# Adding a kernel's residual input by an accumulating DMA, and starting the B and C products one slot earlier

## The chip, the cores and the metric

The kernel runs on one core of a Trainium2 chip. The metric is the device time of one execution in microseconds (us). A core has five engines that run their own queues in order: TensorE (PE in the profile, with PEld for its weight loads), VectorE (DVE), ScalarE (ACT), GpSimd (POOL) and SyncE (SP), which here only issues transfers. They meet at semaphores.

## The reference

The input `x` has the shape (4, 512, 64, 64) in float32: 4 batches, 512 channels, 4096 positions. Two layers follow each other, each of the form `x = x + layer(group_norm(x))`:

```python
# layer 0: mamba
xn = layer_norm(gn(x))                      # tokens of 512 channels, as 4 chunks of 128
xi, z = split(in_proj(chunk))               # 256 inner channels
xc = silu(causal_conv4(xi) + conv_b)
dt, B, C = x_proj(xc);  dt = softplus(dt_proj(dt) + dt_b)
h[t] = exp(dt[t] * A) * h[t-1] + dt[t] * xc[t] * B[t]      # 256 channels x 16 states
y = ((h * C).sum(states) + xc * D) * silu(z)
x = x + proj(layer_norm(out_proj(y) + skip * chunk)) + proj_b
# layer 1: linear attention, 8 heads
q, k, v = qkv(gn(x));  q, k = relu(q), relu(k)
kq = k.T @ q;  x = x + out_proj(v @ kq / kq.sum())
```

The addition that the change is about is the first `x +` (line "x = x + proj(...)"): the input of layer 0 is added to the projection's output. The group norm of layer 1 needs mean and variance of each channel of the sum over all positions, so statistics of the sum are collected as it is made.

## The kernel before

**Tiling.** The positions of a batch are cut into 8 tiles of 512 (index t), the channels into 4 chunks of 128 (index c). One *step* is a batch, tile and chunk: 128 steps. A step has 16 *slots* (index s), 2048 in all. In each slot `slot` (L578 on) writes out: on GpSimd the product `bx` for the slot after next (`drive`, L584), on VectorE two scans along the 512 positions (L602), each on 128 rows that hold 32 channels by 4 states, on ScalarE two exponentials `dA` for the scans to come (`decay`, L576), and on VectorE the product of the states with C for the first 384 positions (`product`, L625). Every second slot GpSimd copies the states on (L612) and multiplies the last 128 positions (L613), and TensorE makes the next `c_all` (the C values spread over the rows, `c_row`, a matmul into the only bank of its pool) and sums the states into `y` (`fold_states`).

**Pieces.** Everything else is cut into generators, and `after()`, at the end of each slot, lets some of them go on by a piece. The order is written by this loop when the program is built, not found at run time. `later(n, what)` issues `what` n slots later; `pause(n)` and `until(...)` yield until then. The queues `ahead` (layer norm of the next tile), `late` (the projection of the tile before) and `rest` (attention of the batch before) advance as long as a credit of TensorE work allows: 3.5 units a slot, a unit being a matmul of 512 columns in float32; `mm` counts them, bfloat16 as a quarter, and four small ones side by side as one.

**Banks.** The pool `ps_w` has 4 PSUM banks, used in rotation by all these pieces (`work_bank`). A matmul into a bank waits until the last reader of the tile before in that bank is done.

**Projection.** `projected` (L413 on), one call per tile, runs mostly in the slots of the steps with c = 2 and 3. After the layer norm it takes a tile buffer, one of three, and loads the 1 MiB of `x` into it from DRAM over SyncE (`load_x`, L130, tile name `xr`). For each of the 4 output chunks o it issues 4 matmuls with `w_pr` into a bank `pp` and then the *fold*: four 32x32 matmuls with an identity (`fold`) side by side, which add `xr` into the same bank. Two slots later ScalarE copies the bank plus bias over `xr` (L421), and a slot after that VectorE takes `bn_stats` of it (L423). Then the tile is stored to a DRAM tile `x1` (L442).

**Mixers.** `mixers` makes a step's B, C and time values from the SiLU output: one bank `pd` with two matmuls, the copy `dtr` and the bfloat16 `parts` (L518, L526), then twice a small correction matmul on the same bank and a copy (L531). These are six pieces; the last one reads `pd` for the last time. In before they run in slots 12 to 15 of one step and slots 0 and 1 of the next. In slot 1 `time_banks` issues the two matmuls `pt`, which need two banks, and in slot 2 ScalarE does the softplus. In slot 10 ScalarE does the SiLU of the step after next, with a table load on either side.

Of the kernel before, what the change touches and what calls it, by code (L numbers as in the profile page):

```python
# [8 lines left out]
F32 = mybir.dt.float32  # L9
BF16 = mybir.dt.bfloat16  # L10
AF = mybir.ActivationFunctionType
ALU = mybir.AluOpType
AX = mybir.AxisListType

P = 128
T = 512
# [8 lines left out]
def kernel(  # L25
# [24 lines left out]
    nc = tc.nc  # L50
    B, C, L = x.shape
    NC = C // P
# [6 lines left out]
    BLK = 32  # L59
# [6 lines left out]
    wk = ctx.enter_context(tc.tile_pool(name="wk", bufs=2))  # L66
# [19 lines left out]
    def later(n, what):  # L86

        done = []

        def both():  # L90
            what()
            done.append(True)

        if now[0] is None:
            both()
        else:
            due.append((now[0] + n, both))
        return done

    def until(*done):  # L100
        while not all(done):
            yield "wait"

    def pause(n):
        return until(later(n, lambda: None))
# [8 lines left out]
    def cols(v, b):  # L114
        return v[b].rearrange("(c p) l -> p c l", p=P)

    def mm(out_, lhsT, rhs, abreast=1, **how):

        work["mm"] += (0.25 if rhs.dtype == BF16 else 1.0) * rhs.shape[-1] / T / abreast
        nc.tensor.matmul(out_, lhsT, rhs, **how)  # L120
# [3 lines left out]
    def no_tile(spare=0):  # L124
        return now[0] is not None and held_x[0] + spare >= TILES

    def load_now(src, name):
        held_x[0] += 1
        xt = wk.tile([P, NC, T], F32, tag="x", name=name, bufs=TILES)
        nc.sync.dma_start(xt, src)  # L130
        return xt

    def load(src, name):

        while no_tile():
            yield "wait"
        return load_now(src, name)

    TILES = 3
    held_x = [0]  # L140
# [4 lines left out]
    def load_x(b, t, why):  # L145
        return load(cols(x, b)[:, :, t * T : (t + 1) * T], f"x{why}_{b}_{t}")
# [26 lines left out]
    for i in range(1, 4):  # L173
        r = slice(i * LANE, (i + 1) * LANE)
# [10 lines left out]
    fold = const.tile([P, BLK], F32, tag="fold", name="fold")  # L185
    for k in range(KS):
        r = slice(k * BLK, (k + 1) * BLK)
# [47 lines left out]
    for e in range(NH):  # L235
        r = e * (LANE + NST)
# [25 lines left out]
    for i in (2, 3):  # L262
        r = slice(i * LANE, P)
# [16 lines left out]
    for o in range(NC):  # L280
        pw = work_bank(f"pw_{o}")
        for c in range(NC):
            mm(
                pw[:, 0:1], w_pr[:, c, o * P : (o + 1) * P], b_sb[:, c : c + 1],
                start=(c == 0), stop=(c == NC - 1),
# [127 lines left out]
    def projected(ym, stats, x1, b, t):  # L413

        nm = f"{b}_{t}"
        yield from layer_norm(ym, f"b_{nm}", False)
        xt = yield from load_x(b, t, "r")
        taken = []

        def take(o, pp):  # L420
            nc.scalar.activation(xt[:, o, :], pp, AF.Identity, bias=pb[:, o : o + 1])  # L421
            free()
            later(1, lambda: nc.vector.bn_stats(stats[:, o, t, :], xt[:, o, :]))  # L423

        for o in range(NC):
            yield from room()
            pp = work_bank(f"pp_{nm}_{o}")
            for c in range(NC):
                mm(
                    pp, w_pr[:, c, o * P : (o + 1) * P], ym[:, c, :],  # L430
                    start=(c == 0), stop=False,
                )
                if c == 1:
                    yield "more"
            for k in range(P // BLK):
                r = slice(k * BLK, (k + 1) * BLK)
                mm(pp[r, :], fold[r, :], xt[r, o, :], abreast=P // BLK, start=False, stop=True)
            taken.append(later(2, lambda o=o, pp=pp: take(o, pp)))
            yield
        yield from until(*taken)  # L440
        yield from pause(1)
        nc.sync.dma_start(x1, xt)  # L442
        later(2, free_x)

# [520 lines left out]
    with tc.manual_schedule():  # L965
        credit, seen, mix, held[0], held_x[0] = 0.0, work["mm"], iter(()), 0, 0
        for n, (b, t, c) in enumerate(steps):
            f, nm = fs[n], names[n]
            before = fs[n - 1] if n else None
            nxt = fs[n + 1] if n + 1 < N else None  # L970
            front = step_inputs(n + 2) if n + 2 < N else iter(())
            last_mix, mix = mix, mixers(fs[n + 2], names[n + 2]) if n + 2 < N else iter(())
            if c == 0 and (t + 1 < NT or b + 1 < B):
                add_to(ahead, tile_norm(b, t + 1) if t + 1 < NT else tile_norm(b + 1, 0))
            if c == 0 and t == 0 and b + 1 < B:
                add_to(light, input_norm(b + 1))
            assert c != 2 or not ahead
            for s in range(SLOTS):
                def after():
                    nonlocal credit, seen  # L980
                    now[0] = n * SLOTS + s
                    for what in [w for at, w in due if at <= now[0]]:
                        what()
                    due[:] = [d for d in due if d[0] > now[0]]
                    if s == 0 and before is not None:
                        take_y(before, n - 1, 1)
                    if s == SLOTS // 2:
                        take_y(f, n, 0)
                    if s < 2:
                        next(last_mix, None)  # L990
                    if s == 1:
                        spread(f, 1, nm)
                        if before is not None:
                            gate(before, 1)
                        if nxt is not None:
                            time_banks(nxt, names[n + 1])
                    if s == 2 and nxt is not None:
                        nc.scalar.preload_act_table_set("softplus")
                        time_steps(nxt, names[n + 1])
                        nc.scalar.preload_act_table_set("natural_log_exp_and_others")  # L1000
                    if s == 5 and before is not None:
                        pb_, pt_, pc_ = steps[n - 1]
                        with_skip(before, xn[pb_, pt_], pc_)
                        if pc_ == NC - 1:
                            add_to(late, leave(pb_, pt_))
                    if s in (2, 4, 5, 6, 7, 8):
                        next(front, None)
                    if s == 3 and nxt is not None:
                        to_rows(nxt, 0, names[n + 1])
                        to_rows(nxt, 1, names[n + 1])  # L1010
                    if s == 3 and before is not None:
                        pb_, pt_, pc_ = steps[n - 1]
                        out_proj(before, xn[pb_, pt_], pc_, names[n - 1])
                    if s == 9:
                        gate(f, 0)
                        if nxt is not None:
                            spread(nxt, 0, names[n + 1])
                    if s == 10 and n + 2 < N:
                        silu(n + 2)
                        nc.scalar.preload_act_table_set("natural_log_exp_and_others")  # L1020
                    if s >= 12:
                        next(mix, None)
                    may = [
                        what for k, what in ((0, "wide"), (1, "one ahead"), (2, "two ahead"))
                        if any(a - 2 * k <= s <= a - k for a in AWAY) or (k == 2 and s >= SLOTS - 2)
                    ]
                    if light and light[0][1] == "wait" or s in AWAY and not any(
                        q and q[0][1] == "wide" for q in (ahead, late)
                    ):
                        one(light)  # L1030

                    limit[0] = 3 if 9 <= s < 13 else 2
                    credit = min(credit + 3.5 - (work["mm"] - seen), 2.6)
                    busy = False
                    for queue in (ahead, late, rest):
                        kind = queue[0][1] if queue else None
                        if queue is ahead or kind == "free" or credit > 0 or kind == "more" and not busy:
                            start = work["mm"]
                            one(queue, ANYWHERE if queue is ahead and (c, s) > (1, 4) else may)
                            credit -= work["mm"] - start  # L1040
                            busy = busy or work["mm"] - start > 1
                    seen = work["mm"]

                slot(n * SLOTS + s, N * SLOTS, after)
            fs[n - 1].clear() if n else None
        product(N * SLOTS - 1, N * SLOTS)
        now[0] = None
        for _, what in due:
            what()
# [60 lines left out]
```

## Time and profile before

| | |
|---|---|
| time, median of 3 runs | 8276.37 us (8275.0 to 8279.44) |
| profiled run: span, mean granted TensorE clock | 8268.9 us, 0.885 |
| loads of `xr` | 32 of 1 MiB, by SyncE |
| copies L421, statistics L423 | 128 each, median 684 ns and 668 ns |
| DMA queues in use | hardware_dynamic and instruction only |

Busy time is the union of an engine's instructions; an engine in order is idle between two instructions either because it waits for a semaphore or because it has nothing. The profile names for each idle stretch the instruction, on whichever engine, that ended it ("releaser"). A name such as `h<-dA,st,bx` tells what an instruction writes and reads, by the program's own tile names with numbers left out. All matmuls have the line L120, that of the helper `mm`, so they are told apart by tiles.

### The profile page before, as it was taken

The page shows a single profiled execution, that of the slowest core. Times are in us where ns is not written, and L with a number is a line of the kernel's source. Part 1 is how long each engine was busy: PE and PEld are TensorE (multiplying, and loading weights), DVE is VectorE, ACT ScalarE, POOL GpSimd, SP SyncE. Part 2 cuts the span into 40 slices and gives each one's busy share as a digit, 9 for nine tenths or more (in the row PEclk, how much of TensorE's full clock was granted, in tenths as well). Part 3 has the DMA queues.
Part 4 walks back from the last instruction along what each step waited for, and adds up shares of the span by engine and source line. Part 5 has one row for each costly group of instructions (what it writes and reads, how often), then busy time and mean ns, then how long its engine had stood idle before and what let it go on. Part 6 is the DMA issues. An engine that isn't in the chain of part 4 may idle for free. (4 is left out here: it accounts for less than half of the span.)

```text
span 8268.9 us, 89639 instructions
## 1 busy us (share of the span) xinstructions
PE 6698.2 (81%) x23450; PEld 2248.1 (27%) x23520; DVE 7187.9 (87%) x6890; ACT 5366.3 (65%) x7841; POOL 6856.1 (83%) x4565
## 2 busy tenths in 40 slices
PE   5677777767788888888788888888788888888699
PEld 1122222112222222322222222232223223233244
DVE  5999999999999999988999999988889999998700
ACT  4666666666666776666677766667667666666421
POOL 4999899999888888888888988888889888888600
PEclk8788888778899989999899999899889999989799
DMA  5666665666666666666666666566666655666412
GB/s 159 165 162 160 146 152 144 155 148 159 164 162 151 155 161 151 161 177 169 165 153 161 164 160 160 149 161 179 161 154 157 156 144 148 152 175 180 120 39 87
DMA packets 829317, 1266.32 MB, mean 153 GB/s; under 512 B 183920, under 2 KB 317568, under 8 KB 816512
## 3 DMA queue, kind: packets, MB, share of 16 engines
q1 hardware_dynamic: 821632, 1255.87, 60.3%
q10 hardware_dynamic: 7168, 4.71, 0.2%
q8 instruction: 184, 3.01, 0.2%
q14 instruction: 333, 2.73, 0.1%
HBM read 1053.28 MB, written 206.57 MB: 152 GB/s over the span
## 5 line engine op out<-in xcount | busy, mean ns | idle before, releaser
L584 POOL TENSOR_TENSOR bx<-d_all,b_all 128x1024 f32<-128x1024 f32 x2048 | 4793.8, 2360 | 98.7 <-DVE h L602 82.1
L602 DVE TENSOR_TENSOR_SCAN h<-dA,st,bx 128x512 f32<-128x512 f32 x3584 | 4432.6, 1269 | 236.4 <-ACT dA L576 141.8
L576 ACT ACTIVATE dA<-d_all,a_t 128x512 f32<-128x512 f32 x4096 | 2803.6, 689 | 2227.3 <-DVE h L602 2202.4
L625 DVE TENSOR_TENSOR h<-h,c_all 128x768 f32<-128x768 f32 x2048 | 1909.2, 932 | 256.0 <-PE c_all L120 246.1
L613 POOL TENSOR_TENSOR h<-h,c_sb 128x512 f32<-128x512 f32 x1024 | 1298.2, 1268 | 110.4 <-DMA c_sb<-c_rows 18.3
L120 PE MATMUL y<-h,fold 128*32 128x512 f32 x8192 | 1278.2, 700 | 122.7 <-POOL h L613 118.7
L120 PE MATMUL c_all<-parts,sel 128*128 128x384 bf16 x1024 | 374.2, 365 | 1097.2 <-DVE h L625 1094.7
L120 PE MATMUL pq<-w_qk,xa 128*128 128x512 f32 x2048 | 1039.8, 640 | 10.7 <-issue 5.1
L120 PE MATMUL pc<-xn,w_cv 128*128 128x512 f32 x2048 | 1015.5, 626 | 39.9 <-ACT res L850 15.6
L612 POOL COPY st<-h 128x4 f32<-128x4 f32 x1024 | 192.7, 188 | 631.1 <-DVE h L602 583.5
L602 DVE TENSOR_TENSOR_SCAN h<-dA,bx 128x512 f32<-128x512 f32 x512 | 602.7, 1209 | 93.3 <-ACT dA L576 84.4
L120 PEld LDWEIGHTS <-sel 128*128 128x128 bf16 x1280 | 127.7, 100 | 1864.8 <-DVE h L625 1632.3
L120 PEld LDWEIGHTS pc<-xn,w_cv 128*128 128x128 f32 x2048 | 377.8, 197 | 698.9 <-issue 564.0
L120 PEld LDWEIGHTS pq<-w_qk,xa 128*128 128x128 f32 x2048 | 411.4, 205 | 496.2 <-issue 472.9
L120 PE MATMUL pr<-xb,m 128*128 128x512 f32 x1024 | 514.5, 641 | 7.9 <-ACT parts L531 5.9
L120 PE MATMUL pp<-xn,w_pr 128*128 128x512 f32 x1024 | 516.3, 630 | 3.8 <-DVE xn L387 3.8
L120 PE MATMUL pt<-dt,w_dt 32*128 32x512 f32 x512 | 270.7, 885 | 108.1 <-ACT parts L531 55.0
L120 PEld LDWEIGHTS y<-h,fold 128*32 128x32 f32 x8192 | 171.0, 114 | 665.9 <-issue 343.9
L120 PE MATMUL y<-xz,dg 128*128 128x512 f32 x512 | 344.6, 763 | 0.0
L649 POOL TENSOR_TENSOR xz<-xz 128x512 f32<-128x512 f32 x256 | 325.2, 1270 | 2.7 <-ACT xz L646 2.7
L494 POOL TENSOR_TENSOR dt<-dt,xz 128x1024 f32<-128x1024 f32 x128 | 302.6, 2364 | 20.7 <-DMA c_rows<-dt 20.7
L120 PE MATMUL pd<-xz,w_xp 128*128 128x512 f32 x512 | 293.1, 702 | 7.8 <-ACT xz L919 7.8
(156 smaller groups left out, 6141.9 us busy)
## 6 DMA issues: line engine op xcount, KB each, us to landing
d_all<-d_rows SPq DMA_DIRECT2D x2048, 256.0 KB, 6.6
b_all<-b_rows SPq DMA_DIRECT2D x4096, 64.0 KB, 2.2
d_rows<-dt SPq DMA_DIRECT2D x256, 512.0 KB, 2.8
c_sb<-c_rows SPq DMA_DIRECT2D x4096, 16.0 KB, 1.8
xs<-in_x_dram SPq DMA_DIRECT2D x32, 1024.0 KB, 6.8
xn<-in_x_dram SPq DMA_DIRECT2D x32, 1024.0 KB, 6.1
xr<-in_x_dram SPq DMA_DIRECT2D x32, 1024.0 KB, 6.1
x<-xr SPq DMA_DIRECT2D x32, 1024.0 KB, 4.3
```

What stands on the lines that cost most here:

```text
L120: nc.tensor.matmul(out_, lhsT, rhs, **how)
L494: nc.gpsimd.tensor_tensor(f["both"][:, 1], f["both"][:, 0], f["xz"][:, 0], ALU.mult)
L576: nc.scalar.activation(dAs[k], fs[n]["d_all", e][:, 0, j, :], AF.Exp, scale=a_t[:, e, j, q : q + 1])
L584: nc.gpsimd.tensor_tensor(bxs[g], fs[n]["d_all", e][:, 1, jj * 2 : jj * 2 + 2, :], bc(b_all[g // JJ], 2), ALU.mult)
L602: nc.vector.tensor_tensor_scan(h[:, j, :], dAs.pop(2 * g + i), bxs[g][:, i, :], 0.0 if t == 0 else st[:, c, e, q, j : j + 1], ALU.mult, AL ...
L612: nc.gpsimd.tensor_copy(st[:, c, e, q, :], h[:, :, T - 1])
L613: nc.gpsimd.tensor_tensor(h[:, :, CUT:], h[:, :, CUT:], bc(c_sb.pop(g // JJ), NJ), ALU.mult)
L625: nc.vector.tensor_tensor(own, own, bc(c_all[g // JJ], 2), ALU.mult)
L649: nc.gpsimd.tensor_tensor(f["xz"][:, 1, e, :], f["xz"][:, 1, e, :], f["xz"][:, 0, e, :], ALU.mult)
```

## The change

The input is no longer loaded ahead and added by TensorE. `projected` takes the tile buffer without a load (`new_tile`), TensorE does only the 16 matmuls with `w_pr`, ScalarE copies the four banks plus bias into the buffer, and then one transfer issued by GpSimd reads `x` from DRAM and adds it to what stands in the buffer (`accum_op=ALU.add`). The statistics need the sum, so they move behind that transfer: four slots later, two in one piece and two in the next, and the store follows them. It is for taking the folds off TensorE and the wait for the load out of its queue. Besides, the six pieces of `mixers` begin in slot 11 in place of 12, and so end in slot 0 in place of 1.

```diff
+    def new_tile(name):
+        held_x[0] += 1
+        return wk.tile([P, NC, T], F32, tag="x", name=name, bufs=TILES)
+
     def load_now(src, name):
-        held_x[0] += 1
-        xt = wk.tile([P, NC, T], F32, tag="x", name=name, bufs=TILES)
+        xt = new_tile(name)
         nc.sync.dma_start(xt, src)
         return xt
...
-        xt = yield from load_x(b, t, "r")
+        while no_tile():
+            yield "wait"
+        xt = new_tile(f"xr_{nm}")
         taken = []
 
         def take(o, pp):
             nc.scalar.activation(xt[:, o, :], pp, AF.Identity, bias=pb[:, o : o + 1])
             free()
-            later(1, lambda: nc.vector.bn_stats(stats[:, o, t, :], xt[:, o, :]))
...
-                    start=(c == 0), stop=False,
+                    start=(c == 0), stop=(c == NC - 1),
                 )
                 if c == 1:
                     yield "more"
-            for k in range(P // BLK):
-                r = slice(k * BLK, (k + 1) * BLK)
-                mm(pp[r, :], fold[r, :], xt[r, o, :], abreast=P // BLK, start=False, stop=True)
             taken.append(later(2, lambda o=o, pp=pp: take(o, pp)))
             yield
         yield from until(*taken)
-        yield from pause(1)
+
+        nc.gpsimd.dma_start(xt, cols(x, b)[:, :, t * T : (t + 1) * T], accum_op=ALU.add)
+        yield from pause(4)
+        for o in range(NC):
+            nc.vector.bn_stats(stats[:, o, t, :], xt[:, o, :])
+            if o % 2:
+                yield
         nc.sync.dma_start(x1, xt)
         later(2, free_x)
...
-                    if s < 2:
+                    if s < 1:
                         next(last_mix, None)
...
-                    if s >= 12:
+                    if s >= 11:
                         next(mix, None)
```

## The prediction

> **What bounds the kernel now.** I read the busy table and the costliest groups first, then busy time by stretch, then the waits of VectorE inside the loop, and then the tiles `xr` and `pt` that the change touches.
>
> From the page, one total and two groups (busy us, mean ns of one, then idle before and its releaser):
>
> ```profile
> PE 6698.2 (81%) x23450; PEld 2248.1 (27%) x23520; DVE 7187.9 (87%) x6890; ACT 5366.3 (65%) x7841; POOL 6856.1 (83%) x4565
> ...
> L584 POOL TENSOR_TENSOR bx<-d_all,b_all 128x1024 f32<-128x1024 f32 x2048 | 4793.8, 2360 | 98.7 <-DVE h L602 82.1
> L602 DVE TENSOR_TENSOR_SCAN h<-dA,st,bx 128x512 f32<-128x512 f32 x3584 | 4432.6, 1269 | 236.4 <-ACT dA L576 141.8
> ```
>
> The totals mix two stages. The scans run from 122.5 to 7807 us; after them comes a tail with hardly any VectorE. Busy time in these two stretches (length, then busy us of PE, PEld, DVE, ACT, POOL; granted clock, DMA share, GB/s):
>
> ```profile
> 122.50:7807.00 7684.50, 6206.76 (x21809) 2025.51 (x21863) 7119.94 (x6730) 5235.89 (x7647) 6840.93 (x4546) 0.88 0.64 159
> 7807.00:8268.00 461.00, 436.68 (x1524) 199.31 (x1540) 29.63 (x76) 97.03 (x150) 3.72 (x4) 0.94 0.16 57
> ```
>
> In the loop VectorE works 7119.94 of 7684.50 us, 92.7%: it is the bound, and all that the loop can give is its idle 565 us. GpSimd follows with 6840.93 us. A loop of 2048 slots makes a slot 3.75 us, of which GpSimd uses 3.34. What VectorE's idle time waits for (us, times, longest):
>
> ```profile
> DVE h L625 <- PE c_all L120: 246.1, 114, 11.2
> DVE h L602 <- ACT dA L576: 177.1, 171, 6.4
> DVE h L602 <- issue: 55.0, 37, 3.2
> DVE h L602 <- POOL h L613: 25.1, 25, 2.4
> ```
>
> The largest is TensorE handing over `c_all` late. I took these 114 waits one by one and found the slot of each by counting scans: 86.5 us at slot 3, 91.8 at slot 7, 57.2 at slot 15, 9.3 at slot 9; 168 of the 246 us are in steps with c=2, where `projected` runs. Two causes return. From the answers on `xr` and on `pt`, TensorE idles until:
>
> ```profile
>   DMA xr<-in_x_dram: 78.5, 32
> ...
>   ACT parts L531: 131.7, 47
> ...
> DMA to landing us min/median/max: 3.8/5.9/10.8
> ```
>
> Two stretches of the timeline show each reaching VectorE:
>
> ```profile
> 3851.99 1.93 PE L120 MATMUL pp<-xr,fold 32*32 32x512 f32 x8 [7.15 <-DMA xr<-in_x_dram]
> 3857.66 0.95 DVE L625 TENSOR_TENSOR h<-h,c_all 128x768 f32<-128x768 f32 x1 [11.19 <-PE c_all L120]
> ...
> 4283.38 1.67 PE L120 MATMUL pt<-dt,w_dt 32*128 32x512 f32 x2 [2.61 <-ACT parts L531]
> 4289.11 0.95 DVE L625 TENSOR_TENSOR h<-h,c_all 128x768 f32<-128x768 f32 x1 [3.82 <-PE c_all L120]
> ```
>
> In the first, the fold of the input stands in TensorE's queue ahead of `c_all` and waits for its load. In the second, `pt` needs the PSUM bank that `pd` gives back only after the copy at L531, issued in the same slot.
>
> **What the Trainium skill says.** "DMA: Bandwidth & Descriptors", section "SWDGE vs HWDGE vs iDMA": an accumulating transfer goes by GpSimd alone, whose processors write the descriptors before any byte moves. No queue of that kind is in the page of before, so its trace can't confirm it. The same page, "Anatomy of one DMA — SWDGE (gpsimd) path", fits 2.0 us plus bytes/436e3: by that an estimate of 4.4 us for 1 MiB, alone and not accumulating; the trace's plain loads by SyncE take 5.9 us median beside the loop's traffic. "SBUF — State Buffer", section "Who interferes with whom": such a transfer starves when VectorE holds the shared port. The loop's scan and product take one tensor from PSUM (`dA`, `c_all`), so I expect little of it.
>
> **The change part by part.**
>
> *Folds leave TensorE.* 16 small matmuls per tile, four side by side: the timeline has 8 in 1.06 us, so 2.1 us per tile and 68 us over 32 tiles. TensorE isn't the bound, so this is worth nothing by itself. The attention pieces that fill TensorE end before the loop does in both programs (I counted them in the order of each), so the tail keeps the same attention, all of the last batch's. And the order of the changed program puts six `pp` matmuls (3.6 us) where four and a fold (2.4 + 0.6) stood, in slots 6 and 7 of c=2, in 10 tiles: the wait at slot 7 grows by 0.6 us there, **+6 us**.
>
> *No load ahead of the fold.* Of the VectorE waits for `c_all`, 18 (80.6 us) follow a TensorE wait for `xr`. Taking in each the smaller of the two waits leaves 29.6 us at slot 15 and 16.3 at slot 7: **-46 us**.
>
> *The mixers' six pieces run in slots 11 to 15 and 0.* 18 VectorE waits at slot 3 (51.9 us) follow a `pt` that waits for L531; the smaller of each pair sums to 47.7 us. With the four banks in rotation, the order of before has 79 `pt` banks last read in the slot in which `pt` is issued, and that of the changed program 1. So **-48 us**. At slot 11 `pd` needs the SiLU issued in slot 10; in the timeline TensorE reaches that place some 5 us after the SiLU ends, because the slot's own fold is ahead of it: nothing added.
>
> *Adding transfer on GpSimd.* Behind it in that queue are `bx` of the slot after next and the next tail product, for which VectorE and TensorE wait. It waits for the last ScalarE copy (L421, 684 ns), issued in the same slot, while `st` and the tail product (0.19 + 1.27) run: about nothing, except at slot 11, behind SiLU and table loads, some 3 us. For writing the descriptors I have only prices: low 1 us (the skill's first-byte latency for this path, section "Specifications"), high 4 us, four times that, an estimate since a row here is 2 KB in four pieces per partition. I take 2. GpSimd is two slots ahead (7.5 us), and until the next `bx` it needs 1.27 + 2.36, so about 3.9 us of delay are free, and it regains 0.4 us in each slot. **0 us**, at the high end with slot 11's wait about 3 us in nine tiles, 27.
>
> *Statistics wait for the landing.* `bn_stats` keeps its number (128 of 668 ns) and moves four slots behind the transfer's issue, 15.0 us. The wait is VectorE's own, with every scan behind it. Bounds for the landing: the plain load's median 5.9 us, and twice its longest, 21.6 us, if the adder must read two streams. I take 10, plus 2 for descriptors: 12 us, inside the 15. Let one tile in four run 2 us over: **+16 us**.
>
> *The tail.* There nothing hides the transfer. The last copy comes 2.1 us earlier, then 12 us of transfer and four statistics of 0.67 us in a row, where before the last copy was followed at once by one statistic and L299; the attention of the last batch starts with it. -2.1 + 12 + 2.0 is **+12 us**.
>
> Sum: -46 - 48 + 6 + 16 + 12 = -60 us: 8276 - 60 = **8216 us**, 0.7% faster.
>
> **The rivals.** *The landing replaces the waits removed (slower).* If adding takes 18 us with descriptors 2, the 31 tiles in the loop overrun by 5 us each: +155 in place of +16, tail +20 in place of +12, so 8276 - 88 + 155 + 20 = 8363. For it: the DMA share in the loop is 0.64 already, and loads that move as much as this take up to 10.8. Against: those 10.8 are the worst of 32. A blocked GpSimd gives the same order: 8 us of descriptors, 3.9 free, 4.1 x 31 = 127: 8276 - 88 + 127 + 12 = 8327. *The gain is given back on TensorE (no change).* The credit that the folds no longer use calls other fillers into the same slots, ScalarE's wait for `dA` (177 us) takes over, and half of the 94 us remains: 8276 - 47 + 6 + 16 + 12 = 8263, and within 0.2% with little more. For it: the order shows the +0.6 us above. Against: a `pt` that no longer waits can't be filled up again.
>
> **How the numbers follow.** Forecast 0.58, between 8180 and 8255; no change 0.14; slower 0.28, of which most at 8300 to 8370. Faster 0.58, same 0.14, slower 0.28. The low end takes a landing that never overruns and a slot 7 that doesn't grow, 8276 - 94 + 12 = 8194, less a margin of 14 us for other waits on `pt` (62.4 us for `res`, in the same answer) that the other order of banks may shorten: 8180. The high end is the slower rival with a margin cut where 1 in 10 is left out, 8355.
>
> **What would show it.** Right: no TensorE wait for `xr`; the waits of `pt` for L531 gone; VectorE's wait for `c_all` near 150 us; waits for the landing below 20 us; a tail 12 us longer. Wrong: the first `bn_stats` of a tile waits for DMA for some us in most tiles, or the scan waits for `bx` after each adding transfer.

## The result and the profile after

| | before | after |
|---|---|---|
| time, median | 8275.69 us (4 runs) | 8354.08 us (8344.8 to 8364.17, 4 runs) |
| ratio to before, 95% interval | | 1.0095 (1.0078 to 1.0113) |
| profiled span | 8268.9 us | 8349.7 us |
| first scan to end of the last | 7684.5 us | 7760.3 us |
| end of the last scan to the end | 461.9 us | 464.8 us |

The kernel became 78 us slower; 60 us faster was forecast. (In the printed code `slot` begins at L588, not at the L578 named ahead of it.) Of the 80.8 us that the profiled span grew, 75.8 lie in the loop, 2.9 in the tail and 2.2 ahead of the loop.

From the page of after: the busy totals, the group of the scans, the new queue (packets, MB, share of 16 engines), and the issues of the adding transfer (KB each, us to landing).

```profile
PE 6613.6 (79%) x22496; PEld 2221.2 (27%) x22496; DVE 7199.0 (86%) x6890; ACT 5374.9 (64%) x7841; POOL 6901.0 (83%) x4597
...
L609 DVE TENSOR_TENSOR_SCAN h<-dA,st,bx 128x512 f32<-128x512 f32 x3584 | 4438.5, 1269 | 387.5 <-ACT dA L583 196.3
...
q0 software_dynamic: 16896, 33.56, 2.3%
...
xr<-in_x_dram POOLq DMA_DIRECT2D x32, 1024.0 KB, 10.3
```

TensorE lost 85 us of work and nobody gained by it. A scan takes the same 1269 ns, but the idle time before the scans of this group rose from 236.4 to 387.5 us. The loop and the tail by stretches, with the columns of the prediction:

```profile
124.65:7884.90 7760.25, 6127.97 (x20871) 2001.87 (x20871) 7132.00 (x6730) 5244.44 (x7647) 6883.88 (x4576) 0.88 0.65 157
7884.90:8349.00 464.10, 428.47 (x1508) 195.53 (x1508) 28.83 (x77) 97.08 (x150) 5.08 (x5) 0.94 0.17 59
```

VectorE works 7132 us in the loop, 12 more than before, and idles 628 in place of 565. VectorE's waits in the loop of after:

```profile
DVE h L609 <- ACT dA L583: 274.2, 187, 51.3
DVE h L632 <- PE c_all L120: 124.2, 69, 10.0
DVE h L609 <- issue: 95.3, 47, 3.8
DVE h L609 <- POOL h L620: 92.7, 52, 3.2
```

The wait for `c_all` fell from 246.1 to 124.2 us: what the change was to take away, it took away. (The first row holds also a wait of 51.3 us ahead of the loop.) In its place come scans that wait, under several names. Counting scans again to place every idle stretch in the slot of the last scan ahead of it, the loss has one place (by this count "slot 13" holds the idle time ahead of the first scan of slot 14, whose `dA` is issued in slot 13):

| VectorE idle in the loop, us | before | after |
|---|---|---|
| slot 3, for `c_all` | 86 | 18 |
| slot 7, for `c_all` | 92 | 86 |
| slot 11, all | 115 | 116 |
| slot 13, all | 5 | **190** |
| slot 15, for `c_all` | 57 | 5 |
| for the landing of `xr` | 0 | 6 |

Slot 13 had been nearly free of waits; after, its idle time goes under `POOL h L620` (85 us), issue (83) and `POOL st L619` (16). The timeline of after there, for one step (a float32 matmul has two records in these traces, so the two of `pd` count as 4):

```profile
2620.83 1.93 PE L120 MATMUL y<-h,fold 128*32 128x512 f32 x8 [0.56 <-POOL h L620]
...
2622.69 2.63 PE L120 MATMUL pd<-xz,w_xp 128*128 128x512 f32 x4
...
2625.40 0.58 ACT L525 COPY dt<-pd 64x512 f32<-64x512 f32 x1 [1.65 <-POOL bx L591]
...
2626.06 1.27 POOL L620 TENSOR_TENSOR h<-h,c_sb 128x512 f32<-128x512 f32 x1
...
2627.30 1.29 ACT L583 ACTIVATE dA<-d_all,a_t 128x512 f32<-128x512 f32 x2
...
2628.07 1.28 DVE L609 TENSOR_TENSOR_SCAN h<-dA,st,bx 128x512 f32<-128x512 f32 x1 [2.35 <-POOL h L620]
```

Read from the bottom. The scan starts as the first of the two `dA` becomes ready, so it waits for ScalarE, whatever releaser the bracket names. ScalarE had been idle 1.65 us, until 2625.40, and then had the two copies of `pd` and part of a layer norm to do before that `dA`. And 2625.40 is when the matmuls of `pd` are through (2622.69 + 2.63), on TensorE behind slot 11's fold, which waits for GpSimd. The copy is issued in slot 12 now, a slot (3.75 us) earlier than before, but its input hardly follows: counted from the end of slot 11's last scan, `pd` is done after 7.7 us in before and after 6.4 us in after (medians over the steps), so 1.3 us earlier. The releasers by name (`bx`, the tail product) are here only those that came last by the records: GpSimd's last tail product ahead of the scan (2626.06 + 1.27) had ended 0.74 us before the scan started. Nearly all steps show the same: of the 94 scans that waited at this place, 92 start within 0.1 us of the end of their own `dA`, and of the 100 copies that waited, 98 start within 0.15 us of the end of a matmul of `pd`.

ScalarE's idle time ahead of that copy, over all steps, is the number behind the second bar of its group (what follows are the releasers). Before:

```profile
L518 ACT COPY dt<-pd 64x512 f32<-64x512 f32 x128 | 73.5, 574 | 33.8 <-PE pd L120 16.9 <-DMA c_sb<-c_rows 5.2 <-POOL h L613 5.1
```

After:

```profile
L525 ACT COPY dt<-pd 64x512 f32<-64x512 f32 x128 | 73.9, 577 | 198.9 <-PE pd L120 101.1 <-POOL st L619 34.9 <-POOL bx L591 34.2
```

That is 165 us more idle time ahead of a copy that isn't on the bound engine, and 185 us more on VectorE at the next slot. On the two resources that the prediction had watched, the answers for `pt`, `xr` and the transfer of after read:

```profile
  ACT parts L538: 28.6, 34
...
  DMA xr<-in_x_dram: 33.0, 4
...
DMA to landing us min/median/max: 9.0/10.3/16.1
```

TensorE's waits of `pt` for the last copy fell from 131.7 to 28.6 us; TensorE has no wait for `xr` left; the 33.0 us are VectorE's, and 26.9 of them are the one in the tail.

### The profile page after: what moved, and what is told of

Read it like the earlier page. It is cut to its first block, busy times and chain, and to the rows that moved or that the text cites. A ratio compares the mean times of both kernels' runs of the same rounds, so it can differ in the third digit from the quotient of the medians.

```text
span 8349.7 us, 87546 instructions
## 1 busy us (share of the span) xinstructions
PE 6613.6 (79%) x22496; PEld 2221.2 (27%) x22496; DVE 7199.0 (86%) x6890; ACT 5374.9 (64%) x7841; POOL 6901.0 (83%) x4597
## 3 DMA queue, kind: packets, MB, share of 16 engines
q0 software_dynamic: 16896, 33.56, 2.3%
## 5 line engine op out<-in xcount | busy, mean ns | idle before, releaser
L609 DVE TENSOR_TENSOR_SCAN h<-dA,st,bx 128x512 f32<-128x512 f32 x3584 | 4438.5, 1269 | 387.5 <-ACT dA L583 196.3
L632 DVE TENSOR_TENSOR h<-h,c_all 128x768 f32<-128x768 f32 x2048 | 1909.2, 932 | 134.1 <-PE c_all L120 124.2
L120 PE MATMUL y<-h,fold 128*32 128x512 f32 x8192 | 1316.1, 719 | 194.0 <-POOL h L620 188.4
L620 POOL TENSOR_TENSOR h<-h,c_sb 128x512 f32<-128x512 f32 x1024 | 1299.7, 1269 | 143.4 <-DMA c_sb<-c_rows 40.2
L120 PE MATMUL pq<-w_qk,xa 128*128 128x512 f32 x2048 | 988.0, 612 | 1.1 <-ACT xa L328 1.1
L619 POOL COPY st<-h 128x4 f32<-128x4 f32 x1024 | 205.2, 200 | 521.2 <-DVE h L609 496.7
L120 PEld LDWEIGHTS pq<-w_qk,xa 128*128 128x128 f32 x2048 | 393.3, 196 | 488.8 <-issue 469.4
L120 PE MATMUL pp<-xn,w_pr 128*128 128x512 f32 x1024 | 484.6, 600 | 9.4 <-ACT xr L426 4.9
L120 PE MATMUL pd<-xz,w_xp 128*128 128x512 f32 x512 | 374.9, 872 | 7.8 <-ACT xz L926 7.8
L120 PE MATMUL pz<-xn,w_z 128*128 128x512 f32 x512 | 292.3, 655 | 3.9 <-ACT xz L466 3.3
## 6 DMA issues: line engine op xcount, KB each, us to landing
xr<-in_x_dram POOLq DMA_DIRECT2D x32, 1024.0 KB, 10.3
```

The costliest lines, as they stand in the source:

```text
L609: nc.vector.tensor_tensor_scan(h[:, j, :], dAs.pop(2 * g + i), bxs[g][:, i, :], 0.0 if t == 0 else st[:, c, e, q, j : j + 1], ALU.mult, AL ...
L619: nc.gpsimd.tensor_copy(st[:, c, e, q, :], h[:, :, T - 1])
L620: nc.gpsimd.tensor_tensor(h[:, :, CUT:], h[:, :, CUT:], bc(c_sb.pop(g // JJ), NJ), ALU.mult)
L632: nc.vector.tensor_tensor(own, own, bc(c_all[g // JJ], 2), ALU.mult)
```

## The experiments

Two theories at first. The *copy theory*: the loss is ScalarE's copy of `pd` in slot 12. The *transfer theory*: the loss comes with the adding transfer on GpSimd, as the releaser `POOL h L620` says. Ratios are to runs of before on the same chip.

**1. Only the adding transfer** (`e1_transfer_only`): the mixers back in their old slots.

```diff
-                    if s < 1:
+                    if s < 2:
                         next(last_mix, None)
...
-                    if s >= 11:
+                    if s >= 12:
                         next(mix, None)
```

> The changed kernel with the mixers back in slots 12 to 15, 0 and 1, so only the adding transfer remains. Copy theory (the time lost is ScalarE's copy of pd, which moved to slot 12 and there waits for TensorE): the 185 us of VectorE idle that the change brought at slot 13 vanish, the waits for xr stay away, slot 3 is as before; 8276 - 46 - 9 + 3, about 8225 us. Transfer theory (the loss comes from GpSimd's issue of the adding transfer, since the profile names the tail product on GpSimd as releaser at slot 13): the loss stays and the gain at slot 3 goes, 8354 + 48, about 8400 us.

8272.53 us, ratio 0.9994 (0.9986 to 1.0002). The idle time at slot 13 is 8 us: the loss isn't the transfer's. But the forecast gain isn't there either. VectorE's waits, of the whole span:

```profile
DVE h L632 <- PE c_all L120: 217.0, 121, 4.9
DVE st L446 <- DMA xr<-in_x_dram: 42.6, 9, 25.6
```

The longest wait for `c_all` is 4.9 us in place of 11.2, and slot 15 has 16 us in place of 57. But slot 7 stays at 93, slot 3 has 100 in place of 86 (though all idle time at slot 3 together is 191 us, as before), and 17 us of waits for the landing are new in the loop (the other 25.6 are in the tail). Together VectorE's idle time in the loop falls by 9 us, from 565 to 556.

**2. Only the mixers moved** (`e2_mixers_only`), on the kernel before.

```diff
-                    if s < 2:
+                    if s < 1:
                         next(last_mix, None)
...
-                    if s >= 12:
+                    if s >= 11:
                         next(mix, None)
```

> The kernel before with only the mixers moved to slots 11 to 15 and 0. Copy theory: VectorE idles about 190 us at slot 13 in place of 5, less up to 48 at slot 3: between 8380 and 8450 us. Transfer theory: only the gain at slot 3, about 8228 us.

8383.34 us, ratio 1.0131 (1.0115 to 1.0146). Slot 13 idles 179 us, slot 3 waits 18 us for `c_all`. Without any adding transfer the copy's row shows the same idle time as after:

```profile
L518 ACT COPY dt<-pd 64x512 f32<-64x512 f32 x128 | 73.8, 576 | 185.2 <-PE pd L120 110.5 <-POOL bx L584 24.8 <-POOL st L612 24.2
```

**3. `pd` early, its copies late** (`e3_copies_at_13`): which half of the move costs?

```diff
-                    if s < 1:
+                    if s < 2:
                         next(last_mix, None)
...
-                    if s >= 11:
+                    if s in (11, 13, 14, 15):
                         next(mix, None)
```

> The changed kernel with the two matmuls of pd still in slot 11, but the copies in slot 13 and the rest in slots 14, 15, 0 and 1 as in before. Copy theory: no loss at slot 13, and no gain at slot 3 either, within 15 us of the run with only the transfer, about 8225 us. A third theory, that the early matmuls of pd are what delays the fold and c_all behind them: the loss stays, about 8390 us. Transfer theory: about 8400 us.

8275.88 us, ratio 1.0 (0.9991 to 1.0008). Slot 13 idles 8 us, ScalarE hardly waits for `pd`, and the early matmuls by themselves cost nothing that can be measured:

```profile
L525 ACT COPY dt<-pd 64x512 f32<-64x512 f32 x128 | 73.2, 572 | 9.4 <-PE pd L120 5.3 <-issue 3.9 <-DMA c_sb<-c_rows 0.2
```

It is the copies' slot that costs. The run lies 50 us above the number expected, as the first one does, since both rest on a transfer worth 52 us.

**4. From slot 12 to slot 0** (`e4_twelve_to_zero`): keep both gains by doing two pieces in slot 15.

```diff
-                    if s >= 11:
+                    if s >= 12:
                         next(mix, None)
+                    if s == 15:
+                        next(mix, None)
```

> The changed kernel with pd in slot 12 and its copies in slot 13, as before, but the first correction's copy and the second correction's matmul both in slot 15, so that the last copy is in slot 0. Copy theory: keeps both gains, 8225 - 48, about 8180 us, or up to 40 us more if TensorE waits in slot 15 for the copy issued just before its matmul. Transfer theory: about 8354 us.

8270.68 us, ratio 0.9995 (0.9987 to 1.0003): a miss by 90 us. Slot 13 idles 11 us and slot 3 waits 20 us for `c_all`, so at these two places the kernel does what the theory says. But slot 1, with 3 us in before and 6 in after, idles 76 us. From the answer on `pd`, TensorE's idle time ahead of a matmul into it:

```profile
  ACT parts L538: 304.3, 121
```

TensorE waits 2.5 us in the mean for the copy issued just before its matmul, and the next `c_all` and fold stand behind that matmul. The copy of `pd` in slot 0 isn't what suffers: all copies L538 together wait 6.8 us for TensorE. It is the copy ahead of it in ScalarE's queue, `xz<-y` (L653), which reads what that fold has summed. ScalarE's idle time ahead of it, in after and in this run:

```profile
L653 ACT COPY xz<-y 128x512 f32<-128x512 f32 x256 | 148.9, 582 | 75.1 <-PE y L120 74.3
...
L653 ACT COPY xz<-y 128x512 f32<-128x512 f32 x256 | 149.2, 583 | 184.9 <-PE y L120 184.5
```

So it is the kind of fault seen in slot 12, at another copy: ScalarE waits for a late TensorE, and `dA` stands behind. This is read from the trace; no run tests it by itself.

**5. `pd` ahead of slot 11's `c_all`** (`e5_pd_before_c_all`): the slots of after, but the matmuls of `pd` issued ahead of slot 11's product, and so of its `c_all` and fold.

```diff
-    def slot(g, last, after):
+    def slot(g, last, after, early):
...
+        if g % SLOTS == 11:
+            next(early, None)
         if g % SLOTS in BEHIND:
             product(g, last)
...
-                    if s >= 11:
+                    if s >= 12:
                         next(mix, None)
...
-                slot(n * SLOTS + s, N * SLOTS, after)
+                slot(n * SLOTS + s, N * SLOTS, after, mix)
```

> The changed kernel, with the same slots for the mixers, but the two matmuls of pd are issued ahead of slot 11's product and its c_all and fold in place of behind them, so that TensorE does them in the idle time before that c_all. Copy theory: ScalarE's copy in slot 12 finds pd ready, the 171 us of late scans at slot 13 vanish and the gain at slot 3 stays: 8354 - 171 + 10, about 8195 us. Rival (a pd that waits for the SiLU now holds c_all itself): VectorE waits about 1 us more for c_all in each of 128 steps, about 8320 us.

8199.61 us, ratio 0.9907 (0.9892 to 0.9922): faster than both kernels. The timeline of this run at the same place of a step:

```profile
2546.70 1.91 ACT L928 ACTIVATE xz<-xz 128x2048 f32<-128x2048 f32 x1
...
2548.67 1.98 PE L120 MATMUL pd<-xz,w_xp 128*128 128x512 f32 x4 [0.41 <-ACT xz L928]
...
2550.94 0.34 PE L120 MATMUL c_all<-parts,sel 128*128 128x384 bf16 x1 [0.29 <-DVE h L634]
...
2554.66 0.57 ACT L525 COPY dt<-pd 64x512 f32<-64x512 f32 x1
2555.12 0.47 ACT L533 CAST parts<-pd 128x384 bf16<-128x384 f32 x1
```

`pd` starts 0.06 us after the SiLU ends and is done at 2550.65, before the product that `c_all` waits for (0.29 us of TensorE idle by VectorE). The copy finds its bank filled. In the median `pd` is done 2.2 us after slot 11's last scan, in place of 6.4. Slot 13 idles 27 us in place of 190, slot 3 waits 19 us for `c_all`.

**6. The same without the transfer** (`e6_mixers_only_pd_before_c_all`): the edit of run 5 and `s < 1` for the last piece, on the kernel before.

> The kernel before with only the mixers moved, and pd issued ahead of slot 11's product as in the run before this one: no adding transfer. Copy theory: 8276 - 68 at slot 3 + 10, about 8220 us. Rival: about 8340 us. The difference to the run before it is what the adding transfer is worth beside mended mixers; expected about 25 us.

8256.99 us, ratio 0.9975 (0.9967 to 0.9983). The mixers so mended bring 21 us; 55 were expected. Slot 3 gives its 68 us, but slots 1, 13 and 15 take back 21, 15 and 15. Between runs 6 and 5 the adding transfer is worth 57 us, though 4 us in run 1: in run 5, VectorE waits 15 us for `c_all` at slot 15 in place of 72, 79 at slot 7 in place of 100, and only 5 us for landings in the loop. Why the two parts together bring more than one by one was not taken apart further; which pieces fall into which slot differs among these programs.

**7. Two slots for the landing** (`e7_transfer_pause_2`), on run 1.

```diff
-        yield from pause(4)
+        yield from pause(2)
```

> The run with only the transfer, with the statistics two slots behind the issue of the transfer in place of four. Prices the landing: 1.3 us on GpSimd and 10.3 us to land, against 2 slots of 3.75 us, leave some 3 to 4 us of VectorE wait in each of 31 tiles, 8273 + 110, about 8380 us. Rival (the statistics are near nothing that waits, the loop catches up): under 8300 us.

8430.71 us, ratio 1.0189 (1.0175 to 1.0203). This is 51 us above the expectation, for the waits are longer than the 3 to 4 us expected (why was not examined). VectorE waits at the statistics in nearly every tile:

```profile
DVE st L446 <- DMA xr<-in_x_dram: 209.9, 31, 26.5
```

Without the longest, in the tail, that is 183 us in the loop, 6.1 us in each of 30 tiles, and the time grew by 158 us over run 1. These are 166 us more of waits than in run 1, so a wait of VectorE for a landing was paid nearly in full here.

**8. Six slots for the landing** (`e8_transfer_pause_6`), on run 1: `pause(6)`.

> The run with only the transfer, with the statistics six slots behind the transfer in place of four. The 17 us of VectorE waits for the landing inside the loop should go: about 8258 us. Rival (the tile buffer held two slots longer keeps attention from its loads, other waits take the place): 8273 us or more.

8252.57 us, ratio 0.9978 (0.9969 to 0.9986). No wait for a landing remains in the loop, and 20 us are gained over run 1, within the noise as much as the 17 us of these waits.

**9. Both mended** (`e9_both_mended`): run 5 with `pause(6)`.

> The version with pd ahead of slot 11's product and the adding transfer, and the statistics six slots behind the transfer. If each wait is worth its own length: that version has only 5 us of VectorE waits for the landing inside the loop left, so 8195 us, not to be told from it. If what six slots brought the run with only the transfer (20 us) lies in the later place of the statistics and not in the landing: about 8180 us.

8215.52 us, ratio 0.9927 (0.9914 to 0.9941). Its interval meets that of run 5 (0.9892 to 0.9922): no gain, and the profiled run is rather slower. It has no landing waits in the loop, but VectorE's idle time in the loop is 506 us where run 5 has 479, with more of it in slots 1, 2 and 11. So the first expectation is the nearer one, though 20 us too low, and that the 20 us of run 8 were the landing's alone isn't shown. Run 5 stays the best version.

## Why the prediction was wrong

Its step "the mixers' six pieces" failed, and there the clause that ends in "nothing added". It looked for a wait of TensorE for the SiLU at slot 11, saw in the timeline that TensorE reaches that place late, behind the slot's own fold, and concluded that nothing waits. The same sight has a second half: if `pd` doesn't come a slot earlier too (it came 1.3 us earlier), what reads `pd` and does move by a slot has to wait. The copies L525 and L533 moved from slot 13 to 12, into a queue in which `dA` for the next scans stands behind them. That costs 185 us at slot 13, where the prediction had 0; runs 1 and 3 (copies back) and 5 (`pd` really earlier) take it away, and run 2 has it without the transfer. Neither rival had it: the time of the slower one, 8363 us, lies near the measured 8354, but for another cause, a late landing, which took 6 us in the loop.

The other terms, forecast and measured by slot in after:

| term | forecast, us | measured, us |
|---|---|---|
| bank of `pt` free a slot earlier, `c_all` at slot 3 | -48 | -68 |
| copies of `pd` a slot earlier, slot 13 | 0 | **+185** |
| no load ahead of the fold, `c_all` at slot 15 | -30 | -52 |
| the same and six matmuls of `pp`, `c_all` at slot 7 | -16 + 6 | -6 |
| statistics wait for the landing | +16 | +6 |
| the tail | +12 | +3 |

The measured terms sum to +68, of the 78 by which the kernel became slower. Outside of them are 12 us of further busy time on VectorE and changes of other waits in both directions. One goes against the first row: scans at slot 3 waited 13 us more, so that slot as a whole gained 55 us, not 68.

The price of the transfer was near, though with some luck. The landing was taken as 10 us with 2 for the descriptors; the trace has 10.3 in the median from the start of the issue, 1.3 of them the issue on GpSimd, whose queue waited for the ScalarE copies 43.8 us in all, 37.2 of that in the tail. But the 10 was put between bounds from an answer on the tile `xr` that holds the loads and the stores of that tile together. The page of before has them apart:

```profile
xr<-in_x_dram SPq DMA_DIRECT2D x32, 1024.0 KB, 6.1
x<-xr SPq DMA_DIRECT2D x32, 1024.0 KB, 4.3
```

So the plain load takes 6.1 us in the median, not 5.9, and the 3.8 and 10.8 are stores'; of the 23 loads whose landing the trace has, the longest took 8.1. The Trainium skill, "DMA: Bandwidth & Descriptors", section "SWDGE vs HWDGE vs iDMA", has such a transfer on GpSimd alone; the trace shows it there, 32 x 1 MiB in a queue of its own, and no run shows whether another engine could issue it. In the tail the wait was there, 26.9 us of VectorE with 9.1 from issue to statistics, and up to the first `pq` with `w_qk` the tail grew by 8 us. From there to the end the attention took 404.3 us (before 409.5; why was not examined), so the tail as a whole grew by 3 us only.

A second error hides behind the first. The adding transfer alone should bring 12 us by the prediction's terms (-46 + 6 + 16 + 12) and 52 by the expectation of run 1; it brings 4 when run by itself, and its interval holds a ratio of 1. The waits for `c_all` fell by 29 us where the terms have 40: by 41 at slot 15, more than the 30 forecast, but not at slot 7 (93 us in place of 92), where 16 were forecast, and at slot 3 they grew by 14. The landings cost 17 us, as forecast, and the tail 2 in place of 12. The time is near that of the rival "given back on TensorE"; which work of TensorE took what the load had left was not examined.

## What to carry to other kernels

When a piece is issued earlier, go through everything that the move takes along, and ask of each instruction whether its input comes as much earlier; if not, it carries a wait into its queue, and what counts is who stands behind it there. An idle place of the bound engine with several releasers by name is best laid on a time axis: here three names at one place in the step were one cause. And a producer is moved earlier by its place in its engine's queue, ahead of what waits there, not by the slot number that it is issued in.

## What the runs showed of the hardware

An adding transfer of 1 MiB from DRAM into SBUF took 1.3 us on GpSimd to issue and 10.3 us in the median to land beside this traffic (9.0 to 16.1), where the plain load by SyncE of the kernel before took 6.1. It took 2.3% of the 16 DMA engines' time for 32 transfers, under a queue of its own, `software_dynamic`, with 16896 packets for 33.56 MB. With four slots of 3.75 us between its issue and its reader, 5 to 21 us of waits were left in the loop in all (runs 1, 3, 4 and 5, and after); with two, 6.1 us in each of 30 tiles; with six, none.
